# Moving a mixture-of-experts layer's row gathers between the dense matmul stages, and its bias loads into the first pass

## The chip, the cores and the metric

The kernel runs on one core of one Trainium2 chip. The metric is the time on the device in microseconds (us), as the median of three runs. A separate execution was recorded by the hardware profiler; it shows each engine's instructions and the DMA queues. In what follows PE is TensorE (matmuls), DVE is VectorE, ACT is ScalarE, POOL is GpSimd and SP is SyncE, which here only issues DMAs.

## The reference

The input `x` is 32 images of 56 x 56 positions with 128 channels, in fp32. Layer 0 adds a binarised 3 x 3 convolution of the group-normalised input to `x`. Layer 1 treats the 3136 positions of an image as tokens: it adds windowed attention (64 tokens a window, 4 heads, causal) of the normalised tokens, and then a mixture-of-experts layer in which each of the 64 experts picks its 8 best tokens of each image. Cut to what matters here:

```python
def _L1_attn_ref(x, w_qkv, w_proj, b_proj):
    qkv = xw @ w_qkv.T                      # windows of 64 tokens, 4 heads of 32
    ...
    attn = jnp.einsum('bhqd,bhkd->bhqk', q, k) * scale
    attn = jnp.where(causal, attn, NEG)
    attn = jax.nn.softmax(attn, axis=-1)
    out = jnp.einsum('bhqk,bhkd->bhqd', attn, v)
    ...
def _L1_ffn_ref(x, gate_w, gate_b, weight1, weight2):   # E = 64, K = 8, H = 512
    logits = jnp.einsum('bsd,ed->bse', x, gate_w) + gate_b
    probs = jax.nn.softmax(logits, axis=1)              # over an image's tokens
    vals, idx = jax.lax.top_k(probs.transpose(0, 2, 1), K)
    ...
    gathered = jnp.take_along_axis(x, flat_idx[:, :, None], axis=1)
    pooled = jnp.einsum('bked,bke->bed', gathered, topv)
    h = jnp.concatenate([pooled.transpose(1, 0, 2), ones], axis=-1)
    h = jax.nn.gelu(jnp.einsum('ebd,edh->ebh', h, weight1), approximate=False)
    h = jnp.concatenate([h, ones], axis=-1)
    out = jnp.einsum('ebh,eho->ebo', h, weight2)
    ...
    outputs = outputs.at[jnp.arange(Bn)[:, None], flat_idx].add(weighted)
```

The last row of each expert's `weight1` (129 x 512) and `weight2` (513 x 128) is the bias that the appended ones multiply.

## The kernel before, in words

**First pass.** SP loads all images, in 16 pairs; PE transposes them and DVE takes the statistics that the normalisations of layer 0 need (`xb`, `pt`, `st`, lines 299 to 312). Small weights are loaded and transposed ahead of it. At its end SP writes zeros to the DRAM tensor `share` (line 318), and a chain on DVE and POOL makes the thresholds `thr_a` and `thr_b` that the first convolution block needs.

**Main loop.** Two images at a time (a pair) go through in 7 blocks of 8 image rows, so 112 blocks. One iteration `n` works on several blocks at once: it runs attention of block `n` (`this`), projects queries, keys and values of `n + 1` (`nxt`), convolves `n + 4` (`conv`), and finishes block `n - 1` (`prev`). The order of the calls in the loop body is the order of instructions on every engine: the kernel declares a manual schedule for PE, DVE, ACT, SP and POOL. In an iteration PE runs, in this order: `scores` (four mask matmuls L599, then 112 small matmuls L610), four taps of the convolution (L517), the transposes L448 of `norm2` and `bits`, queries and keys (L570), `attend` (112 small matmuls L659), the gate (L723), the transposes of `norm1` (L548), `values` (L586), `turn_out` (L682), the other five taps (L517), and `project` (L692). Each small matmul of `scores` and `attend` has a weight load of its own. I call these two the dense stages: 224 instructions each.

ACT follows `scores` with two exponentials (`pT`, L625), and DVE follows `attend` with the reciprocals of the row sums (`rs`, L667). POOL raises variances to a power (L434, for `ln_rstd` and `devs`), stores the finished tokens (`out_dram`, L714), stores `ln_rstd` (`rdev`, L549) and reads it back broadcast over partitions (`rr`, L554), which DVE multiplies in at L561, in the iteration after next.

**Selection.** When a pair's seven blocks are through, its selection follows in steps, one per iteration of the next pair: `steps` holds the pairs and their step `j`. At `j` = 4 `tokens` finds the indices of the best tokens, at `j` = 5 `gather` reads their rows (eight indirect DMAs of 128 rows of 512 bytes, on POOL, L826), at `j` = 6 `row_stats` takes the rows' statistics. Step 5 falls into the fifth block of the following pair. Fifteen pairs are gathered in the loop; the last one in the tail.

**Biases.** In iteration `n` = 14 SP loads `hbias`, the hidden layer's biases, as 128 partitions x 64 experts x 4 numbers (L971), and makes four DRAM-to-DRAM copies that write the output biases, each repeated for 32 images, to `obias_d` (L977). Both are used only in the tail.

**Tail.** The experts' two layers run in eight groups, and the weighted outputs are added to the rows and scattered.

Of the kernel before, what the change touches and what calls it, by code (L numbers as in the profile page):

```python
# [8 lines left out]
F32 = mybir.dt.float32  # L9
# [5 lines left out]
ALU = mybir.AluOpType  # L15
AX = mybir.AxisListType

P = 128
# [3 lines left out]
K = 8  # L22
# [8 lines left out]
def kernel(  # L31
# [15 lines left out]
    nc = tc.nc  # L47
    B, H, W, C = x.shape
    S = H * W
    E, D1, HF = weight1.shape  # L50
# [3 lines left out]
    NHC = HF // P  # L54
    NPAIR = B // 2
    NG = E // (P // B)
    EG = P // B
# [3 lines left out]
    NU = BT // WIN  # L61
# [7 lines left out]
    const = ctx.enter_context(tc.tile_pool(name="const", bufs=1))  # L69
    dram = ctx.enter_context(tc.tile_pool(name="dram", bufs=1, space=bass.MemoryType.DRAM))  # L70
# [2 lines left out]
    share = dram.tile([NQ, P, NPAIR, 2, ES], F32, name="share")  # L73


    start = ExitStack()
    once = start.enter_context(tc.tile_pool(name="once", bufs=1, side="right"))
    ident = const.tile([P, P], F32, name="ident")
# [12 lines left out]
        out=head1, in_=head1, compare_op=ALU.is_ge, fill=0.0, base=0,  # L91
# [3 lines left out]
        out=head1, in_=head1, compare_op=ALU.is_ge, fill=0.0, base=HD - 1,  # L95
# [73 lines left out]
    with tc.tile_pool(name="prep", bufs=1) as prep, tc.tile_pool(  # L169
        name="xs", bufs=3  # L170
# [7 lines left out]
        nc.sync.dma_start(out=wp_in, in_=w_proj)  # L178
        wg_in = prep.tile([E, P], F32, name="wg_in")
        nc.sync.dma_start(out=wg_in, in_=gate_w)  # L180
        wc_in = prep.tile([P, NTAP, P], F32, name="wc_in")
        nc.sync.dma_start(out=wc_in, in_=conv_w.rearrange("kh kw i o -> i (kh kw) o"))

# [48 lines left out]
        wgc = centred(wg_in.unsqueeze(1), "wgc")  # L232
        nc.tensor.transpose(tg, wgc[:, 0, :], ident[:E, :E])
        nc.vector.tensor_copy(gateT, tg)

        wabs = prep.tile([P, NTAP, P], F32, name="wabs")
        nc.scalar.activation(wabs, wc_in, AF.Abs)
# [36 lines left out]
        def group_norm(b0, b1):  # L274

            bs = slice(b0, b1)
            mg_ps = wps.tile([P, B], F32, name="sums")
            nc.tensor.matmul(mg_ps[:, bs], lhsT=g4f, rhs=mean[:, bs], start=True, stop=True)
            nc.vector.tensor_copy(mg[:, bs], mg_ps[:, bs])
            nc.vector.tensor_sub(dev[:, bs], mean[:, bs], mg[:, bs])  # L280
            nc.vector.tensor_mul(v2[:, bs], dev[:, bs], dev[:, bs])
            nc.vector.tensor_add(v2[:, bs], v2[:, bs], var[:, bs])
            sg_ps = wps.tile([P, B], F32, name="signs")
            nc.tensor.matmul(sg_ps[:, bs], lhsT=g4f, rhs=v2[:, bs], start=True, stop=True)
            nc.vector.tensor_scalar(sg[:, bs], sg_ps[:, bs], 1e-5, None, ALU.add)
            nc.gpsimd.tensor_tensor(rg[:, bs], sg[:, bs], nhalf[:, bs], ALU.pow)
# [29 lines left out]
                scaled(0, B - 8)  # L316
        for q in range(NQ):
            nc.sync.dma_start(out=share[q].rearrange("p n i s -> p (n i s)"), in_=zero)
        group_norm(B - 8, B)
        scaled(B - 8, B)  # L320
        bmean = small("bmean", 1)
# [24 lines left out]
    grows = dram.tile([NQ, P, NPAIR, P], F32, name="grows")  # L346
    toks = [dram.tile([2, S, P], F32, name=f"toks{i}") for i in range(NPAIR)]
    eout = dram.tile([E, B, P], F32, name="eout")
    obias_d = dram.tile([P, NG, P], F32, name="obias_d")
    rdev = [dram.tile([P, NU], F32, name=f"rdev{i}") for i in range(NPAIR * NB)]  # L350
    devs = [dram.tile([2, NB * NU, WIN], F32, name=f"devs{i}") for i in range(NPAIR)]


    hbias = const.tile([P, E, NHC], F32, name="hbias")

    class Part:

# [19 lines left out]
    def main_loop(fast):  # L377
        with ExitStack() as main:
# [87 lines left out]
            class Block:  # L466
# [184 lines left out]
                def attend(self):  # L651

                    av = bank2("av")
                    for u in range(NU):
                        for h in range(HEADS):
                            for i in range(2):
                                rows = slice(i * WIN, (i + 1) * WIN)
                                m = u * 2 + h // 2
                                nc.tensor.matmul(  # L659
                                    av[h % 2 * WIN : (h % 2 + 1) * WIN, i, m * VW : (m + 1) * VW],  # L660
                                    lhsT=self.pT[h // 2][rows, h % 2, u, :],
                                    rhs=self.vb[rows, u, h, :],
                                    start=True, stop=True,
                                )
                    a = av[:, :, : 2 * NU * VW].rearrange("p i (m v) -> p i m v", v=VW)
                    rs = w2.tile([P, 2, 2 * NU], F32, name="rs")
                    nc.vector.reciprocal(rs, a[:, :, :, HD])  # L667

                    self.ao = w1.tile([P, NU, 2, 2, HD], F32, name="ao")
                    for i in range(2):  # L670
                        nc.vector.tensor_mul(
                            self.ao[:, :, i],
                            a[:, i, :, :HD].rearrange("p (u m) d -> p u m d", m=2),
                            rs[:, i].rearrange("p (u m) -> p u m", m=2)
                            .unsqueeze(3).to_broadcast([P, NU, 2, HD]),
                        )
# [52 lines left out]
            class Pair:  # L729
# [89 lines left out]
                            out=rowidx[i * ES : (i + 1) * ES, self.pr, :], in_=src[i]  # L819
                        )  # L820

                def gather(self):
                    pr, pairidx = self.pr, self.pairidx
                    self.rows = wp.tile([P, K, P], F32, name="rows")
                    for k in range(K):
                        nc.gpsimd.indirect_dma_start(  # L826
                            out=self.rows[:, k, :], out_offset=None,
                            in_=toks[pr].rearrange("i t c -> (i t) c"),
                            in_offset=bass.IndirectOffsetOnAxis(ap=pairidx[:, k : k + 1], axis=0),
                        )  # L830
# [128 lines left out]
            def at(n):  # L959
                return blocks[n] if 0 <= n < N else None  # L960

            for n in range(-7, N + 1):
# [4 lines left out]
                ends = dict(steps)  # L967
                if at(n + 7):
                    at(n + 7).load()
                if n == N // 8:  # L970
                    nc.sync.dma_start(  # L971
                        out=hbias,
                        in_=weight1[:, C : C + 1, :].rearrange("e o (p c) -> p e (o c)", c=NHC),
                    )

                    for e in range(EG):
                        nc.sync.dma_start(  # L977
                            out=obias_d[e * B : (e + 1) * B],
                            in_=weight2.rearrange("(g e) h o -> e h g o", e=EG)[e, HF : HF + 1]
                            .to_broadcast([B, NG, P]),  # L980
                        )
                if n == N - 3:
                    front.close()
                    late = main.enter_context(
# [18 lines left out]
                    nxt.normalise()  # L1003
                if at(n + 3):
                    at(n + 3).residual()
                if prev:
                    prev.norm2(pairs[prev.pr])
                if at(n + 2):
                    at(n + 2).spread1()
                if 5 in ends:  # L1010
                    ends[5].gather()
                if 7 in ends:
                    ends[7].put_rows()
                if at(n + 6):
# [5 lines left out]
                    pair.step(j)  # L1020
                if this:
                    this.attend()
                if prev:
                    prev.gate_logits(pairs[prev.pr])
                if this and this.r == NB - 1 and n < N - 1:
# [147 lines left out]
            obias = wp.tile([P, S], F32, name="drow")[:, : NG * P].rearrange("p (g o) -> p g o", o=P)  # L1173
            nc.sync.dma_start(out=obias, in_=obias_d)
            load_rows(0, 0, N1)
            pair.gather()
            other.shares(range(0, 8))
            other.store_shares()
            pair.exps()
# [85 lines left out]
```

## Time and profile before

| | us |
|---|---|
| median of 3 runs | 2330.26 |
| lowest and highest | 2326.86 to 2334.21 |
| profiled execution, its own time | 2467.31 |
| its span, first to last instruction | 2465.6 |
| PE busy in the span | 2101.3 |
| DVE busy | 1773.5 |
| ACT busy | 1147.8 |
| POOL busy | 988.5 |

The mean clock granted to TensorE in the profiled execution is 0.938 of full speed. Busy times are sums over the span; an engine can be busy with work that nobody waits for. In the lines quoted below, `x` with a number counts instructions, an arrow names what is written from what is read, and the part in brackets is the idle time before an instruction and what ended it ("issue" where the profile shows nothing that was waited for).

### The profile page before, as it was taken

The numbers are of one execution on the slowest core, as the hardware profiler recorded it, in microseconds if no ns is written. First come the engines' busy times: TensorE is split into PE (matmuls) and PEld (weight loads), VectorE is DVE, ScalarE is ACT, GpSimd is POOL, SyncE is SP. The second block draws the span as 40 slices with busy tenths as digits, with TensorE's granted clock in tenths as the row PEclk, the third lists the DMA queues.
The fourth block names the chain that finished last, engine by engine and source line by source line (L and its number), as shares of the span: only waits on it lengthen the run. The fifth ranks groups of instructions, "written<-read, shape, count | busy, mean of one in ns | idle before, by whom it ended". The sixth has DMA issues, their size and how long they took to land.

```text
span 2465.6 us, 81828 instructions
## 1 busy us (share of the span) xinstructions
PE 2101.3 (85%) x35081; PEld 1465.5 (59%) x35081; DVE 1773.5 (72%) x4974; ACT 1147.8 (47%) x1683; POOL 988.5 (40%) x996
## 2 busy tenths in 40 slices
PE   6768999799999999999999999999999999845442
PEld 5646666566666666666666666666666666523332
DVE  8966676678787878787878787878787878674221
ACT  0015555455555555555555564646565555322110
POOL 1013334243444444444444444444444444333555
PEclk9989999999999999999999999999999999867776
DMA  9973454646363636363636363636363635657762
GB/s 379 386 266 93 110 144 120 131 110 156 103 163 102 164 101 165 102 164 103 163 102 164 101 165 101 165 101 165 101 166 100 166 101 142 217 133 266 268 230 85
DMA packets 252889, 386.03 MB, mean 157 GB/s; under 512 B 56998, under 2 KB 181734, under 8 KB 247270
## 3 DMA queue, kind: packets, MB, share of 16 engines
q1 hardware_dynamic: 210150, 255.48, 36.1%
q0 software_dynamic: 40192, 124.18, 18.5%
q8 instruction: 279, 4.57, 0.8%
q10 hardware_dynamic: 2176, 1.05, 0.1%
q14 instruction: 92, 0.75, 0.1%
HBM read 246.52 MB, written 135.14 MB: 155 GB/s over the span
## 4 chain that ended last, share of the span: by engine, by line
PE 61%; DVE 12%; issue 8%; ACT 8%; POOL 5%; DMA 3%; another core or an unknown queue 2%; SPq 0%; ACTq 0%; POOLq 0%; DVEq 0%
PE pj L692 8%; PE sc L610 7%; PE av L659 6%; PE v_ps L586 6%; PE qT_ps L570 6%; PE kT_ps L570 5%; PE cv L517 4%; ACT aoT L685 4%; PE yt L548 3%; PE lg L723 3%; PE tt L448 3%; DVE st L308 3%; PE xT_ps L448 3%; POOL out_dram L1159 3%; ACT vblk L590 2%
## 5 line engine op out<-in xcount | busy, mean ns | idle before, releaser
L434 POOL TENSOR_TENSOR devs<-ln_var,nhalf 128x7 f32<-128x7 f32 x112 | 178.7, 1595 | 702.1 <-DVE ln_var L431 692.9
L625 ACT ACTIVATE pT<-sc 128x896 f32<-128x896 f32 x224 | 193.7, 916 | 370.4 <-PE sc L610 370.3
L434 POOL TENSOR_TENSOR ln_rstd<-ln_var,nhalf 128x7 f32<-128x7 f32 x112 | 174.4, 1557 | 402.8 <-DVE ln_var L431 402.5
L441 DVE BATCH_NORM_STATS2 ln_st<-tok 128x6 f32<-128x128 f32 x784 | 162.6, 279 | 183.0 <-ACT tok L709 182.7
L517 PE MATMUL cv<-hbits,wconv 128*128 128x448 f16 x1008 | 242.8, 369 | 15.5 <-DVE s L531 9.7
L659 PEld LDWEIGHTS av<-vblk,pT 64*64 64x64 f32 x12544 | 194.6, 135 | 84.5 <-ACT bn L496 68.0
L610 PE MATMUL sc<-qT,kT 32*64 32x64 f32 x12544 | 198.7, 239 | 43.9 <-issue 42.2
L610 PEld LDWEIGHTS sc<-qT,kT 32*64 32x64 f32 x12544 | 169.3, 134 | 98.7 <-issue 98.6
L692 PE MATMUL pj<-aoT,wprojT 64*128 64x448 f32 x896 | 200.3, 566 | 27.7 <-ACT aoT L685 8.9
L659 PE MATMUL av<-vblk,pT 64*64 64x33 f32 x12544 | 207.5, 221 | 11.5 <-issue 10.7
L590 ACT COPY vblk<-v_ps 128x896 f32<-128x896 f32 x112 | 101.6, 907 | 243.4 <-PE v_ps L586 241.2
L488 ACT ACTIVATE xT<-xT_ps,conv_nb 128x896 f32<-128x896 f32 x112 | 114.1, 1019 | 174.9 <-PE xT_ps L448 166.2
L570 PE MATMUL qT_ps<-n1T,wqkvT 128*128 128x448 f32 x448 | 191.9, 552 | 2.9 <-DVE n1T L561 2.7
L586 PE MATMUL v_ps<-wqkvT,n1T 128*128 128x128 f32 x1568 | 193.5, 275 | 0.0
L570 PE MATMUL kT_ps<-n1T,wqkvT 128*128 128x448 f32 x448 | 188.4, 543 | 0.0
L441 DVE BATCH_NORM_STATS2 ln_st<-yt 128x6 f32<-128x128 f32 x784 | 165.5, 281 | 31.8 <-PE yt L548 27.4
L586 PEld LDWEIGHTS v_ps<-wqkvT,n1T 128*128 128x128 f32 x1568 | 185.2, 193 | 0.7 <-issue 0.7
L701 DVE SCALAR_TENSOR_TENSOR tT<-pj,bproj_c,yT 128x448 f32<-128x448 f32 x224 | 142.7, 678 | 48.7 <-PE pj L692 47.7
L714 POOL DMA_DIRECT2D out_dram<-tok x224 | 170.0, 761 | 0.0
L1159 POOL DMA_INDIRECT out_dram<-f_rows,rowidx x128 | 123.9, 968 | 101.6 <-DVE f_rows L1155 65.0
L826 POOL DMA_INDIRECT rows<-toks,pairidx x128 | 138.5, 1082 | 46.0 <-issue 38.1
L727 ACT COPY logits<-lg 128x448 f32<-128x448 f32 x112 | 59.8, 534 | 203.3 <-PE lg L723 203.3
(190 smaller groups left out, 4162.1 us busy)
## 6 DMA issues: line engine op xcount, KB each, us to landing
xb<-in_x_dram SPq DMA_DIRECT2D x16, 3136.0 KB
xb<-in_x_dram SPq DMA_DIRECT2D x224, 224.0 KB
rr<-rdev POOLq DMA_DIRECT2D x112, 448.0 KB
toks<-tok SPq DMA_DIRECT2D x224, 224.0 KB
out_dram<-tok POOLq DMA_DIRECT2D x224, 224.0 KB
u<-in_L_ffn_weight_dram SPq DMA_DIRECT2D x16, 2048.0 KB
drow<-devs SPq DMA_DIRECT2D x94, 224.0 KB
share<-zero SPq DMA_DIRECT2D x8, 1024.0 KB
```

Source lines behind the costliest of these rows:

```text
L434: nc.gpsimd.tensor_tensor(rstd, var, nhalf[:, :n], ALU.pow)
L441: nc.vector.bn_stats(st[:, u, :], src[:, u, :])
L517: nc.tensor.matmul(self.cv[:, :BT], lhsT=wconv[:, t, :], rhs=hb[:, r * RB + kh : r * RB + kh + RB, kw : kw + W], start=(t == 0), stop=(t = ...
L570: nc.tensor.matmul(pp[:, a, :BT], lhsT=wqkvT[:, s, :], rhs=flat[:, a * BT : (a + 1) * BT], start=True, stop=True,)
L586: nc.tensor.matmul(units(vp)[:, u, :], lhsT=self.n1T[:, u, :], rhs=wqkvT[:, 2, :], start=True, stop=True,)
L590: nc.scalar.copy(self.vb[:, :, :, :HD], units(vp).rearrange("p u (h d) -> p u h d", d=HD))
L610: nc.tensor.matmul(tiles[h // 2][part, h % 2, u * WIN : (u + 1) * WIN], lhsT=left[hp, u, part], rhs=right[hp, u, part], start=False, stop= ...
L625: nc.scalar.activation(pT, rows2(sc), AF.Exp, scale=HD ** -0.5)
L659: nc.tensor.matmul(av[h % 2 * WIN : (h % 2 + 1) * WIN, i, m * VW : (m + 1) * VW], lhsT=self.pT[h // 2][rows, h % 2, u, :], rhs=self.vb[row ...
L692: nc.tensor.matmul(pj[:, i, :BT], lhsT=wprojT[rows, g, :], rhs=self.aoT[rows, :, g, :], start=(g == 0), stop=(g == 1),)
L714: q.dma_start(out=to[part, :].rearrange("(u t) c -> t u c", t=WIN), in_=tok[i * WIN : (i + 1) * WIN],)
L1159: put = nc.gpsimd.indirect_dma_start(out=of, out_offset=bass.IndirectOffsetOnAxis(ap=rowidx[:, n, q : q + 1], axis=0), in_=rows[q][:, n, : ...
```

## The change

The eight gathers of step 5 are issued in two groups of four. The first group moves up, ahead of `norm2`, and POOL first runs a new operation `seen` that reads one column of `pT[0]`, so the group can't start before the first exponential of this iteration is done. The second group stands behind `attend`, and its `seen` reads one column of `rs`. In the tail all eight are issued together, without `seen`. The hidden layer's biases are loaded at the start of the first pass as rows of experts, transposed by four matmuls and copied to `hbias`. The four copies to `obias_d` are issued behind the zeroing of `share`. The loop no longer loads either.

```diff
+    obias_d = dram.tile([P, NG, P], F32, name="obias_d")
+    hbias = const.tile([P, E, NHC], F32, name="hbias")
...
+        hb_in = prep.tile([E, P, NHC], F32, name="hb_in")
+        nc.sync.dma_start(
+            out=hb_in.rearrange("e p c -> e (p c)"), in_=weight1[:, C, :]
+        )
         wc_in = prep.tile([P, NTAP, P], F32, name="wc_in")
...
+        th = wps.tile([P, NHC, E], F32, name="th", tag="tw")
+        for c in range(NHC):
+            nc.tensor.transpose(th[:, c, :], hb_in[:, :, c], ident[:E, :E])
+        nc.vector.tensor_copy(hbias.rearrange("p e c -> p c e"), th)
...
         for q in range(NQ):
             nc.sync.dma_start(out=share[q].rearrange("p n i s -> p (n i s)"), in_=zero)
+        for e in range(EG):
+            nc.sync.dma_start(
+                out=obias_d[e * B : (e + 1) * B],
+                in_=weight2.rearrange("(g e) h o -> e h g o", e=EG)[e, HF : HF + 1].to_broadcast([B, NG, P]),
+            )
...
-                    rs = w2.tile([P, 2, 2 * NU], F32, name="rs")
+                    rs = self.rs = w2.tile([P, 2, 2 * NU], F32, name="rs")
...
-                def gather(self):
+                def gather(self, ks, behind=None):
                     pr, pairidx = self.pr, self.pairidx
-                    self.rows = wp.tile([P, K, P], F32, name="rows")
-                    for k in range(K):
+                    if behind is not None:
+                        seen = wp.tile([P, 1], F32, name="seen")
+                        nc.gpsimd.tensor_scalar(seen, behind, 0.0, None, ALU.mult)
+                    if ks[0] == 0:
+                        self.rows = wp.tile([P, K, P], F32, name="rows")
+                    for k in ks:
                         nc.gpsimd.indirect_dma_start(
...
-                if n == N // 8:
-                    nc.sync.dma_start(
-                        out=hbias,
-                        in_=weight1[:, C : C + 1, :].rearrange("e o (p c) -> p e (o c)", c=NHC),
-                    )
-                    for e in range(EG):
-                        nc.sync.dma_start(
-                            out=obias_d[e * B : (e + 1) * B],
-                            in_=weight2.rearrange("(g e) h o -> e h g o", e=EG)[e, HF : HF + 1]
-                            .to_broadcast([B, NG, P]),
-                        )
...
                 if at(n + 3):
                     at(n + 3).residual()
+                if 5 in ends:
+                    ends[5].gather(range(0, K // 2), this.pT[0][:, 0, 0, 0:1])
                 if prev:
                     prev.norm2(pairs[prev.pr])
                 if at(n + 2):
                     at(n + 2).spread1()
-                if 5 in ends:
-                    ends[5].gather()
...
                 if this:
                     this.attend()
+                if 5 in ends:
+                    ends[5].gather(range(K // 2, K), this.rs[:, 0, 0:1])
                 if prev:
                     prev.gate_logits(pairs[prev.pr])
...
-            pair.gather()
+            pair.gather(range(K))
```

More of the change, by code (lines that the diff above doesn't have):

```diff
@@ L348 @@
     eout = dram.tile([E, B, P], F32, name="eout")
-    obias_d = dram.tile([P, NG, P], F32, name="obias_d")
     rdev = [dram.tile([P, NU], F32, name=f"rdev{i}") for i in range(NPAIR * NB)]
     devs = [dram.tile([2, NB * NU, WIN], F32, name=f"devs{i}") for i in range(NPAIR)]
-    hbias = const.tile([P, E, NHC], F32, name="hbias")
     class Part:
```

## The prediction

> **What bounds the kernel now.** I read the page first, for the engine that carries the span:
>
> ```profile
> PE 2101.3 (85%) x35081; PEld 1465.5 (59%) x35081; DVE 1773.5 (72%) x4974; ACT 1147.8 (47%) x1683; POOL 988.5 (40%) x996
> PE 61%; DVE 12%; issue 8%; ACT 8%; POOL 5%; DMA 3%; another core or an unknown queue 2%; SPq 0%; ACTq 0%; POOLq 0%; DVEq 0%
> L826 POOL DMA_INDIRECT rows<-toks,pairidx x128 | 138.5, 1082 | 46.0 <-issue 38.1
> ```
>
> TensorE bounds the span. The gathers (L826) cost 138.5 us of POOL, which is 40% busy, so by their own time they are free. But 8% of the chain is "issue": TensorE stood still and the profile names no releaser. To find where, I cut the loop at the first mask matmul of each iteration (L599 in the timeline) and asked for busy time by stretch. These are five iterations in a row, the third, fourth, fifth, sixth and seventh block of a pair. The columns are length, then PE, PEld, DVE, ACT and POOL busy, then the clock granted:
>
> ```profile
> 984.80:1001.00 16.20, 16.11 (x303) 11.18 (x301) 13.94 (x35) 9.29 (x12) 6.02 (x7) 1.00 0.43 116
> 1001.00:1018.40 17.40, 16.20 (x303) 11.19 (x301) 14.73 (x42) 9.32 (x12) 5.80 (x7) 1.00 0.44 109
> 1018.40:1035.30 16.90, 15.99 (x303) 11.14 (x301) 13.11 (x39) 9.23 (x12) 9.12 (x11) 1.00 0.46 125
> 1035.30:1057.30 22.00, 19.09 (x301) 12.94 (x299) 14.41 (x49) 9.94 (x13) 13.95 (x13) 0.92 0.45 117
> 1057.30:1074.30 17.00, 16.18 (x304) 11.24 (x302) 14.17 (x48) 11.93 (x16) 6.56 (x8) 1.00 0.58 139
> ```
>
> An iteration lasts 16.2 us, with TensorE full. The fourth line lasts 22.0 with no more matmuls and a clock of 0.92. The gathers begin in the iteration before it (POOL 9.12) and end in it. Over the 15 pairs gathered inside the loop this iteration lasts 21.7 to 24.0 us; against 16.2 the 15 add up to 94 us. The timeline shows where the time goes (start, length, engine, line):
>
> ```profile
> 1031.77 0.38 PE L682 MATMUL aoT_ps<-ident,ao 128*128 128x128 f32 x2
> ...
> 1036.11 0.92 PE L610 MATMUL sc<-qT,kT 32*64 32x64 f32 x32
> ...
> 1038.84 0.34 PE L610 MATMUL sc<-qT,kT 32*64 32x64 f32 x5 [0.38 <-issue]
> 1039.60 0.95 POOL L826 DMA_INDIRECT rows<-toks,pairidx  x1 [0.30 <-issue]
> ...
> 1041.11 1.11 PE L610 MATMUL sc<-qT,kT 32*64 32x64 f32 x60 [0.40 <-issue]
> 1042.15 1.67 PE L517 MATMUL cv<-hbits,wconv 128*128 128x448 f16 x4
> ```
>
> Undisturbed, the 112 score matmuls take 1.5 us. Here 32 go through at speed, then 5 or so per 0.74 us (7 per us) while gathers run, then the last 60 at speed once the last gather has ended (1040.55). The scores lose 4.7 us; the rest of the 5.8 is the clock, halved afterwards (the four L517 matmuls take 1.67 against 0.94). Stages of few, long matmuls (L682, L517, L692) keep their times beside the gathers: only the two dense stages, scores (L610) and attend (L659), are open to this.
>
> Last I looked for single long iterations. There is one, 29.7 us from 458.6, behind the loads of the biases (L971, L977):
>
> ```profile
> 466.26 0.89 PE L659 MATMUL av<-vblk,pT 64*64 64x33 f32 x44
> 476.81 2.14 PE L659 MATMUL av<-vblk,pT 64*64 64x33 f32 x68 [9.66 <-issue]
> ...
> 445.01 12.53 SPq L977 DMA_DIRECT2D obias_d<-in_L_ffn_weight_dram  x4
> ...
> 456.00:462.00 6.00, 5.87 (x140) 3.53 (x139) 5.89 (x11) 2.95 (x5) 2.15 (x2) 1.00 0.34 40
> 462.00:468.00 6.00, 5.15 (x65) 3.27 (x63) 3.93 (x15) 5.33 (x7) 2.25 (x2) 1.00 0.66 44
> ```
>
> TensorE stops within attend for 9.7 us. The trace's record of its instruction queue has a block that was due and started only at 474.5. The queues move 40 to 44 GB/s at that time, a tenth of what they move in the first pass. This iteration lost 13.4 us and the one before 1.4: 14.8 together.
>
> **The change, part by part.** The sum is made against the profiled execution, 2467.3 us (span 2465.6). The median of the runs shown is 2330.3, 137 us or 5.6% less; I scale the result by 2330/2467 = 0.944 and return to this gap in the rivals.
>
> *Gathers leave the scores.* Removed per pair: 22.15 (the median) less what remains. That iteration keeps its row statistics (L849, eight of 0.2 us on DVE, which is 14.4 of 22 busy), so I set 16.5: 5.6 us.
>
> *First group, behind the first exponentials.* In the undisturbed iteration that starts at 1018.38 the exponentials run from 1020.75, two of 0.87: the first ends at 1021.6. POOL is idle from 1019.5 to 1025.45 there, so the new POOL operation starts at once. Its row is not in the trace. Below: POOL's memset of one column, 0.10; above: POOL's power on one column, 0.56. I take 0.5, with 0.3 for its wait: 1022.4, and 0.3 more to the first gather. Eight gathers took from 1029.41 to 1040.55, 1.39 each; four end at 1028.0. Attend starts at 1026.03: 32 matmuls at speed to 1026.6, then 7 per us until 0.5 after the last gather (14 by 1028.5), then 66 at 112 per 1.83 us (1.1): it ends at 1029.6 instead of 1027.86. Cost 1.75 us; 0.9 at 1.25 per gather, 2.5 if it starts 0.7 later. The half clock would add 1.2; I leave it out, because attend stopped for 1.3 us at 450.5 and the clock stayed at 1.00.
>
> *What is queued behind it on POOL.* The `devs` power (L434) moves from 1025.45 to 1028.0, then two output stores (1.51) and the broadcast of `rr` (L554), from 1028.5 to 1031.1. Its reader is the product of L561 in the next iteration, at about 1039. A broadcast issued at 531.95 had its last packets at about 536, 4.3 us later; 1035.4 is early enough. ACT must not overwrite `pT`, nor DVE `rs`, until POOL has read them; both have two buffers and are written an iteration later. Cost nothing; if that cover were gone, up to 2.6 us per pair.
>
> *Second group, behind the reciprocals.* `rs` is ready by 1030.0, POOL free at 1031.7, gathers from 1032.9 to 1038.2. The next scores would start at 1036.11 + 1.75 = 1037.9, so their first 32 matmuls cover the rest: 0.3 us. `ln_rstd` and its store end at about 1040.7; the broadcast that needs them comes at about 1047. The 0.7 that the third line above has over 16.2 (ACT's copy of L685 late beside the gathers) stays.
>
> Per pair 5.6 - 1.75 - 0.3 = 3.55; by 15: **-53 us**. The last pair's gather, in the tail, is as before.
>
> A rule speaks against this. The Trainium skill, SBUF — State Buffer, "Who interferes with whom" and the part before it, says that a transfer issued from POOL can't write its descriptors while DVE runs an operation that holds the port they share, and stretches from 0.6 to 3.1 us. The first group lies beside DVE's statistics and bits. At 3.1 each, four end at 1035: attend would lose over 7 us and the gain be gone. The row: gathers beside DVE's L701, L561 and L538 (540 to 544) took 0.94 to 1.29 each, and the longest of all 1.89. I go by the row.
>
> *Biases of the hidden layer.* Instead of 8192 pieces of 16 bytes, 64 rows of 2 KB ahead of `wc_in`, four transposes (0.1 to 0.2 each) and one copy of 256 columns from PSUM (L211, 256 columns: 0.41). They stand right before the first statistics of a pass that DVE bounds (18.96 of 20 us busy from 138 to 158): **+0.8 us**.
>
> *Biases of the output* (L977): the same four copies, now between the zeroing of `share` and the first block's load on SP's queue. What held the instructions up at 466? The Trainium skill, Perfetto Trace Analysis, "DMA Optimizations", says that transfers below 2 KB carry a large overhead each; by this rule the 16-byte pieces are the culprit, and the change wins 14.8 at no cost. In the trace the 16-byte load has landed at 456.6, ten us before the stop; the four copies land at 462.8, 469.5, 472.8 and 475.3. So the stop belongs to the copies, and they only move: **-14.8** here, and about 19 us of copying at the start:
>
> ```profile
> 138.00:158.00 20.00, 16.55 (x116) 13.21 (x116) 18.96 (x37) 0.00 (x0) 0.00 (x0) 0.94 0.96 404
> 163.81 2.79 PE L448 MATMUL xT_ps<-ident,xb 128*128 128x128 f32 x14 [0.56 <-DVE sg L285]
> ...
> 169.00 1.34 ACT L496 ACTIVATE bn<-xT_ps,thr_b,thr_a 128x448 f32<-128x448 f32 x2 [2.79 <-DVE thr_b L339]
> ```
>
> The zeros keep the queue full (404 GB/s) to about 158.7, and the first blocks land by 162, just in time. With the copies between, block 0 lands at 158.7 + 19 + 2 = 180; transposes 1.5 and ACT's copy 1.0 put the first `bn` at 183 instead of 169: **+14 us**. Bounds: +5 if the copies go twice as fast, +22 at 40 GB/s for all of the 1.05 MB.
>
> Sum: -53 + 0.8 - 14.8 + 14 = -53 of 2467; scaled -50, hence 2280.
>
> **The rivals.**
> (1) *The start cost is real and the stalls are not* (slower). Where does the timed run save 137 us? Iterations of 16.2 us hold 16.1 of TensorE; there is little to save. The stalls of the profiled execution (94 + 14.8 = 109 us) would be the place, if starving the matmuls' issue is something that recording them causes. Then moving gathers is worth nothing, no stop is removed, and 14 us come on top: 2330 + 14, up to 22. It decides as soon as less than a quarter of the 53 + 14.8 is in the timed run. Against it: the slow supply follows the gathers to half a us, and the tail (285 us, clock 0.5 to 0.7) can hold a share of the 137.
> (2) *Part of the stalls is in the timed run*: a quarter to a half; the two sides cancel: 2320 to 2337.
> (3) *Attend takes over more*: gathers start later than I think and the half clock comes in: 2.5 + 1.2 per pair instead of 1.75, 15 x 1.95 = 29 more; -53 + 29 = -24, scaled -23: 2307.
>
> **How the numbers follow.** The forecast, with (3) at its edge, has 0.60 and its own range 2252 to 2307 (attend at 0.9 and start at +5 on one side). Rival (2) 0.18, rival (1) 0.22. 0.3%, 7 us, is about what a measurement of this kernel can tell from no change: faster 0.60, same 0.18, slower 0.22. The range 2252 to 2344 leaves out half of (1) and a few in a hundred below.
>
> **What would show it.** After, the sixth iteration of a pair should last about 16.5 with the clock at 1.00, the fifth about 18.6 with attend near 3.6 us; no stop at 466; the first `bn` near 183; the granted clock's mean up by about 0.02. Wrong: scores still in groups of five, an attend of over 6 us, `rr` waited for in L561, or the profiled span 50 us shorter while the timed median has not moved.

## The result, and the profile after

| | us | ratio to before |
|---|---|---|
| before, 20 runs | 2330.27 (2321.77 to 2339.28) | |
| after, 20 runs | 2324.58 (2319.64 to 2331.46) | 0.9976 [0.9966, 0.9985] |
| after, profiled execution, its own time | 2323.97 | |

The change gains 5.7 us, 0.24%, where 50 were forecast. The profiled execution of after agrees with its timed runs; that of before had stood 137 us above its own. First, from the page of after, the same three lines as were shown of before:

```profile
PE 2051.1 (88%) x35085; PEld 1437.5 (62%) x35085; DVE 1774.3 (76%) x4975; ACT 1145.4 (49%) x1683; POOL 997.4 (43%) x1026
PE 60%; DVE 14%; ACT 9%; DMA 6%; issue 5%; POOL 4%; SPq 1%; ACTq 0%; POOLq 0%; DVEq 0%
L846 POOL DMA_INDIRECT rows<-toks,pairidx x128 | 131.6, 1028 | 45.1 <-issue 36.7
```

TensorE has 50 us less of busy time with the same matmuls and four transposes more, and "issue" fell from 8% to 5% of the chain. The POOL line is that of the gathers, now 1.03 us each. The windows of after cut the same five iterations of a pair at the first mask matmul (columns as before). Ahead of them stand two stretches of the start, and behind them the tail from the first matmul of the experts (L1105, `hp`) to the end:

```profile
158.00:170.00 12.00, 4.60 (x32) 3.58 (x32) 8.40 (x27) 0.00 (x0) 2.02 (x2) 0.84 0.63 163
170.00:180.00 10.00, 0.00 (x0) 0.00 (x0) 1.80 (x10) 0.00 (x0) 1.03 (x2) 0.50 0.79 115
...
950.07:966.25 16.18, 16.09 (x302) 11.18 (x300) 13.92 (x35) 9.30 (x12) 5.99 (x7) 1.00 0.43 116
966.25:983.63 17.38, 16.18 (x301) 11.18 (x299) 14.71 (x42) 9.32 (x12) 5.76 (x7) 1.00 0.43 110
983.63:1000.23 16.60, 16.44 (x302) 11.43 (x300) 12.34 (x38) 9.22 (x12) 11.55 (x15) 1.00 0.51 132
1000.23:1016.49 16.26, 16.13 (x302) 11.21 (x300) 15.15 (x50) 9.88 (x13) 11.45 (x11) 1.00 0.57 144
1016.49:1033.41 16.92, 16.11 (x302) 11.21 (x300) 14.08 (x48) 11.90 (x16) 6.50 (x8) 1.00 0.57 145
...
2125.60:2322.20 196.60, 103.36 (x704) 74.55 (x704) 56.90 (x122) 46.35 (x256) 125.23 (x130) 0.76 0.75 264
```

The sixth iteration (1000.23) lasts 16.26 us instead of 22.00, with the clock at 1.00. By the two profiles alone (spans of 2465.6 and 2322.2) the change looks like a gain of 143 us. This is the last of the signs of being wrong that the prediction lists: the profiled span 50 us shorter while the timed median has not moved. Here it is 143 us shorter, and the median moved by 5.7. The timeline says why the reading fails:

```profile
183.19 3.22 PE L463 MATMUL xT_ps<-ident,xb 128*128 128x128 f32 x14 [17.32 <-DMA xb<-in_x_dram]
...
185.91 1.33 ACT L511 ACTIVATE bn<-xT_ps,thr_b,thr_a 128x448 f32<-128x448 f32 x2
...
987.02 0.24 POOL L842 TENSOR_SCALAR seen<-pT 128x1 f32<-128x1 f32 x1 [2.27 <-ACT pT L640]
988.01 1.08 POOL L846 DMA_INDIRECT rows<-toks,pairidx  x1 [0.75 <-issue]
...
990.67 1.07 POOL L846 DMA_INDIRECT rows<-toks,pairidx  x1 [0.30 <-issue]
991.28 2.33 PE L674 MATMUL av<-vblk,pT 64*64 64x33 f32 x112
992.05 0.95 POOL L846 DMA_INDIRECT rows<-toks,pairidx  x1 [0.30 <-issue]
...
2243.57 1.24 DVE L1143 TENSOR_TENSOR os<-op,drow 32x128 f32<-32x128 f32 x4 [0.54 <-PE op L1137]
```

The first group starts at 988.01, as forecast 4.4 us into the iteration, and two of its gathers lie beside `attend` (L674). In the forecast's picture that costs 1.75 us: `attend` stalls, and takes 3.6 us. Here all 112 matmuls go through in one piece, in 2.33 us against about 1.84 undisturbed. So in this execution the gathers cost `attend` 0.5 us. Something else than the change must tell the profile of before from that of after.

### The profile page after: what moved, and what is told of

Its sections match the earlier page's. It is cut to its first block, busy times and chain, and to the rows that moved or that the text cites. A ratio compares the mean times of both kernels' runs of the same rounds, so it can differ in the third digit from the quotient of the medians.

```text
span 2322.2 us, 81869 instructions
## 1 busy us (share of the span) xinstructions
PE 2051.1 (88%) x35085; PEld 1437.5 (62%) x35085; DVE 1774.3 (76%) x4975; ACT 1145.4 (49%) x1683; POOL 997.4 (43%) x1026
## 4 chain that ended last, share of the span: by engine, by line
PE 60%; DVE 14%; ACT 9%; DMA 6%; issue 5%; POOL 4%; SPq 1%; ACTq 0%; POOLq 0%; DVEq 0%
PE pj L707 7%; PE av L674 6%; PE sc L625 6%; PE v_ps L601 6%; PE qT_ps L585 5%; PE kT_ps L585 5%; ACT aoT L700 4%; PE yt L563 4%; PE cv L532 3%; PE lg L738 3%; DVE st L322 3%; PE xT_ps L463 3%; PE tt L463 3%; ACT vblk L605 3%; DVE idx L809 2%
## 5 line engine op out<-in xcount | busy, mean ns | idle before, releaser
L674 PEld LDWEIGHTS av<-vblk,pT 64*64 64x64 f32 x12544 | 197.2, 135 | 76.3 <-ACT bn L511 69.2
L532 PE MATMUL cv<-hbits,wconv 128*128 128x448 f16 x1008 | 232.3, 357 | 10.2 <-DVE s L546 8.6
L605 ACT COPY vblk<-v_ps 128x896 f32<-128x896 f32 x112 | 101.6, 907 | 242.6 <-PE v_ps L601 242.6
L707 PE MATMUL pj<-aoT,wprojT 64*128 64x448 f32 x896 | 200.3, 566 | 17.1 <-ACT aoT L700 5.4
L674 PE MATMUL av<-vblk,pT 64*64 64x33 f32 x12544 | 211.5, 221 | 1.7 <-ACT bn L511 0.6
L625 PEld LDWEIGHTS sc<-qT,kT 32*64 32x64 f32 x12544 | 154.3, 130 | 45.9 <-issue 45.2
L716 DVE SCALAR_TENSOR_TENSOR tT<-pj,bproj_c,yT 128x448 f32<-128x448 f32 x224 | 142.7, 678 | 47.8 <-PE pj L707 47.7
L625 PE MATMUL sc<-qT,kT 32*64 32x64 f32 x12544 | 170.6, 233 | 3.4 <-issue 3.4
L846 POOL DMA_INDIRECT rows<-toks,pairidx x128 | 131.6, 1028 | 45.1 <-issue 36.7
L511 ACT ACTIVATE bn<-xT_ps,thr_b,thr_a 128x448 f32<-128x448 f32 x224 | 150.8, 735 | 0.0
```

The lines of the kernel that those rows point to most:

```text
L511: nc.scalar.activation(bn[:, i].rearrange("c h (g j) -> c h g j", j=NU), units(xT_ps)[:, :, i * WIN : (i + 1) * WIN].rearrange("c j (h g) ...
L532: nc.tensor.matmul(self.cv[:, :BT], lhsT=wconv[:, t, :], rhs=hb[:, r * RB + kh : r * RB + kh + RB, kw : kw + W], start=(t == 0), stop=(t = ...
L605: nc.scalar.copy(self.vb[:, :, :, :HD], units(vp).rearrange("p u (h d) -> p u h d", d=HD))
L625: nc.tensor.matmul(tiles[h // 2][part, h % 2, u * WIN : (u + 1) * WIN], lhsT=left[hp, u, part], rhs=right[hp, u, part], start=False, stop= ...
L674: nc.tensor.matmul(av[h % 2 * WIN : (h % 2 + 1) * WIN, i, m * VW : (m + 1) * VW], lhsT=self.pT[h // 2][rows, h % 2, u, :], rhs=self.vb[row ...
L707: nc.tensor.matmul(pj[:, i, :BT], lhsT=wprojT[rows, g, :], rhs=self.aoT[rows, :, g, :], start=(g == 0), stop=(g == 1),)
```

## The experiments

Theories. **A**: the stalls occur only where an execution is recorded (the reason of the prediction's rival 1). **D**, formed from the first runs: there are two conditions of the machine, and a recorded execution takes what timed runs take in the same one. Below, "quicker condition" means that the kernel before takes about 2330 us in timed runs beside the kernel tested, "slower condition" that it takes 2460 to 2473. The runs fell on five chips: chip 12 was in the quicker condition, chips 7, 1, 10 and 11 in the slower one. By their times the 40 runs of the table above are of the quicker condition too, and the profile of before (2467) is of the slower one. In each cut of a kernel below, `...` stands for lines left out.

**Chip 12: the parts of the change one by one** (before: 2329.57).

e1_gathers: the gathers in two groups alone; both loads of the biases as before.

```diff
+                    ends[5].gather(range(0, K // 2), this.pT[0][:, 0, 0, 0:1])
...
+                    ends[5].gather(range(K // 2, K), this.rs[:, 0, 0:1])
```

> The kernel before with the gathers in two groups alone; the biases stay in the loop. Theory A (the stalls of the scores belong to the recorded execution): the profiled span falls by 90 us or more, the timed run moves by no more than 6 us (2324 to 2331). Theory B (the stalls are in the timed runs too, and the start of the loop takes the gain back in the changed kernel): the timed run falls by 20 us or more, to 2310 or below.

Measured: 2324.37, ratio 0.9982 [0.9971, 0.9992], 5.2 us less. The recorded span is 2321.3, 144 us below that of before. Both numbers are what theory A expected, so by itself this run speaks for A. Of the single long iteration behind the biases this execution's timeline has

```profile
469.83 2.13 PE L661 MATMUL av<-vblk,pT 64*64 64x33 f32 x68 [11.38 <-issue]
```

So the stop that the prediction found there is real in the quicker condition too: this iteration and the one before it take 47.8 us together, in after 33.2.

e2_biases: both moves of the biases alone; eight gathers together, as before (the edit is shown against after).

```diff
                     at(n + 2).spread1()
+                if 5 in ends:
+                    ends[5].gather(range(K))
```

> The kernel before with both bias loads moved to the first pass; the gathers stay in one group of eight. Theory A: the profiled span still has the scores at 6 us per gathered pair, its stop at 466 is gone and its first bn comes at 183 to 186; the timed run is within 4 us of before if the stop within attend is in the timed run, and 14 us slower (2344) if it isn't. Theory B: the timed run is 15 us slower or more, so that the gathers' gain and this make the -6 us of both together.

Measured: 2329.28, ratio 0.9998 [0.9986, 1.001]: no change. Gain and cost cancel: the long iteration is gone (33.2 us for the two), and the first mask matmul starts at 221.4 us instead of 204.1 in e1. This execution is also the nearest to a profile of the old gathers in the quicker condition. The sixth iteration in its windows, and the gathers beside the scores (L625) in its timeline:

```profile
1002.01:1018.52 16.51, 16.38 (x302) 11.40 (x299) 15.23 (x50) 9.85 (x13) 14.55 (x14) 1.00 0.55 144
```

```profile
1002.38 1.00 POOL L846 DMA_INDIRECT rows<-toks,pairidx  x1 [0.30 <-issue]
...
1002.86 1.87 PE L625 MATMUL sc<-qT,kT 32*64 32x64 f32 x112
1003.68 0.95 POOL L846 DMA_INDIRECT rows<-toks,pairidx  x1 [0.31 <-issue]
```

The eight gathers lie where they lay before, beside the scores, and the 112 matmuls take 1.87 us against about 1.5 undisturbed. The iteration lasts 16.5 us, not 22; without any gathers (e6_none below) it lasts 16.24. So of the 5.6 us per pair at most 0.3 was there to win. It also speaks against theory A, which expected scores of 6 us in any recording with the gathers in one group.

e4_spread: after, with the four copies to `obias_d` back in the loop, one each in iterations 16, 23, 30 and 37 (the edit is shown against after).

```diff
-        for e in range(EG):
-            nc.sync.dma_start(out=obias_d[e * B : (e + 1) * B], ...
...
+                if n in OB:
+                    e = OB.index(n)
+                    nc.sync.dma_start(out=obias_d[e * B : (e + 1) * B], ...
```

> The changed kernel with the four copies of the output biases taken out of the start of the loop: one each in iterations 16, 23, 30 and 37. If the 14 to 17 us that the start lost in the profile are in the timed run as well, this is 14 us faster than the changed kernel: 2311 timed, and the first bn at 172 in the profile. If the start cost is only in the recorded execution, 2325. If copies in the loop stop the matmuls wherever they stand, each costs up to 3.5 us and the gain is nil.

Measured: 2315.85, ratio 0.9939 [0.9918, 0.996], 13.7 us less than before and the shortest median of all. The first mask matmul starts at 207.6 instead of 219.5, so the copies at the start cost 12 us; a quarter of them in one iteration costs 1 to 2 us in two of the four iterations (17.36 and 18.38 us against 16.16 and 16.47) and nothing in the others.

e6_none: no gathers in the loop.

```diff
+                    if pr < NPAIR - 1:
+                        nc.gpsimd.memset(self.rows, 0.0)
-                    for k in range(K):
+                    for k in range(K if pr == NPAIR - 1 else 0):
```

> The kernel before without the gathers in the loop: the rows of fifteen pairs are set to zero by one POOL memset in the same place (the last pair still gathers), so the output lacks what those rows give. It bounds what any placing of the gathers can win. Theory A: the timed run falls by less than 6 us although the profiled span loses 90 or more. Theory B: the timed run falls by 20 us or more.

Measured: 2317.72, ratio 0.9959 [0.9943, 0.9974]. All 120 gathers of the loop together cost 11.9 us here (6 to 13 by the interval), 0.1 each. That is the ceiling for any way of moving them in this condition; the two groups of e1 win 5.2 of it.

**Chip 7: before is another kernel here** (before: 2460.21).

b2_before and b3_before are the kernel before, unchanged.

> The kernel before, recorded once more, with nothing changed. With the gathers in one group of eight the kernel of the biases alone had a recorded span of 2331, no more than its timed run, so a third theory (C): the first recorded execution of the kernel before was not like its other executions. C: this span is within 10 us of 2330, the sixth iteration of a pair lasts 16.5 us, the stop within attend is still there. Theory A (recording slows the gathers' neighbours): 2440 to 2470 again, with the scores at 6 us.

> The same kernel a third time, for the spread of recorded executions. Theory C: within 10 us of 2330. Theory A: 2440 to 2470.

Measured: 2458.97 and 2453.74, recorded; the timed runs beside them took 2456 to 2467. Not recorded and yet 130 us longer than on chip 12: theory A falls. Theory C falls with it, since the first recorded execution was like these two. D took shape.

e3_hbias: the hidden layer's biases in the first pass; the four copies of the output biases and the gathers stay as in before.

> The kernel before with the hidden layer's biases loaded and transposed in the first pass, the four copies of the output biases still in iteration 14, the gathers in one group. If the copies are what stops the matmuls, the stop of 13 us stays and the timed run is that of before (2329, within 3). If the 16-byte pieces are, the stop is gone and the timed run is 12 to 15 us faster (2315 to 2318).

Measured: 2454.09, ratio 0.9963 [0.9947, 0.9979], 6.1 us less: neither of the two outcomes that were expected. The long iteration lasts 24.1 us, against 29.5 and 30.3 in the two recordings of before on this chip (29.5 to 34.6 in all six), and TensorE stops for 6.4 us in it, now in the scores:

```profile
465.90 1.25 PE L620 MATMUL sc<-qT,kT 32*64 32x64 f32 x60 [6.42 <-issue]
```

So without the load in 16-byte pieces this iteration is 5 to 6 us shorter than on the same chip before, and the copies alone make the rest of the stop. Whether the pieces hold TensorE up themselves, or only hold up the copies behind them, is not shown: no run has the pieces without the copies.

What ends the stop can be read in the traces. They show the fetches of TensorE's instruction blocks, of 16384 bytes each. In all fifteen recordings that have the four copies in iteration 14, no fetch starts for 18 to 24 us, and TensorE resumes 2.2 to 2.5 us after the next one has started (before: 474.47 and 476.81; e3: 463.48 and 465.90). The longest other pause between two fetches in the loop of before is 14.5 us. So the stop looks like a wait for a late block of instructions. That is read from the traces, not tested, and what delays the fetch is not shown.

e5_twice: before with seven more gathers in each of the 15 pairs.

```diff
+                    if pr < NPAIR - 1:
+                        again = wp.tile([P, K - 1, P], F32, name="again")
+                        for k in range(K - 1):
+                            nc.gpsimd.indirect_dma_start(out=again[:, k, :], ...
```

> The kernel before with seven more gathers behind the eight of each pair in the loop, into a tile that nothing reads. If gathers slow the matmuls beside them in ordinary executions as in the first recorded one, 7 gathers more cost about 5 us a pair: 75 us timed. If each gather costs what taking all eight away won (12 us over 15 pairs, 0.1 us a gather), 7 more cost about 10 us. If nothing, 2330.

Measured: 2610.67, ratio 1.0608 [1.059, 1.0627]: 150.5 us for 105 gathers, 1.43 each, in timed runs. That is twice the 75 us expected where gathers slow the matmuls.

**Chip 1: the changed kernel in the slower condition** (before: 2470.39). a2_after is after, unchanged; b4_before is before; e5b_twice and e6b_none repeat e5_twice and e6_none.

> The changed kernel again, beside the kernel before on the same chip. The kernel before was 2330 us on the chip of the first four experiments and 2460 on that of the second four, and its recorded spans (2466, 2457, 2452) are those of the second. Theory D: there are two conditions of the machine. In the first the gathers don't touch the matmuls, and the change wins 6 us (ratio 0.9976); in the second they do, and the change wins what the prediction's sum said or more: 53 us of the scores, the stop and the tail's pauses stay or go (2460 to 2350 or below, ratio 0.98 or lower). If the kernel before is 2330 here, this is 2324; if 2460, 2310 to 2400.

> The kernel before, recorded on this chip. Theory D: the span is within 10 us of the timed runs of this chip; if these are 2330, the sixth iteration of a pair lasts 16.5 us and the tail from its first hidden layer about 198 us; if 2460, 22 and 236.

> Seven more gathers for each of fifteen pairs, as before: where the kernel before took 2460 they cost 150 us, 1.4 us a gather, as long as a gather lasts. Theory D: where the kernel before takes 2330 they cost 0 to 12 us.

> The kernel before without the gathers in the loop (rows of fifteen pairs set to zero). Where the kernel before took 2330 this won 12 us. Theory D: where it takes 2460, this wins about 95 us from the loop (22.2 to 16.2 us in fifteen iterations) and keeps the tail's pauses: 2365.

Measured: a2_after 2425.05, ratio 0.9803 [0.978, 0.9827], **45.3 us less than before** (a little less of a gain than the 2310 to 2400 expected). b4_before 2469.07, e5b_twice 2622.33 (1.0603 [1.0575, 1.0631]), e6b_none 2369.96 (0.9582 [0.9552, 0.9613]): here the gathers of the loop cost 100 us instead of 12.

e6b_none and e6_none are the same kernel, recorded in both conditions. Their fifteen fifth iterations sum to 240.0 us (slower) and 240.3 (quicker), their sixth to 242.6 and 242.5, and the stop of the biases is in both (51.4 and 51.2 us for the two iterations). Their tails take 246.2 and 198.4. So without gathers the loop is the same in both conditions, and only the tail, with its indirect stores, still differs.

The windows of a2_after are those of after in the other condition, fifth and sixth iteration and the tail:

```profile
1000.12:1023.03 22.91, 19.15 (x301) 12.95 (x299) 14.21 (x40) 9.22 (x12) 16.06 (x18) 0.88 0.42 105
1023.03:1039.73 16.70, 16.57 (x301) 11.24 (x299) 13.56 (x47) 9.85 (x13) 7.46 (x7) 0.96 0.51 128
...
2181.00:2424.10 243.10, 104.95 (x704) 76.50 (x704) 57.09 (x123) 46.56 (x256) 125.66 (x130) 0.69 0.62 213
```

The fifth iteration is 6.3 us longer than in after (it is the longest of the 15; their median is 18.80), and the tail as it is cut here, whose code the change doesn't touch, is 46 us longer with nearly the same busy times. The timeline of a2_after, first with `attend` (L674) in the same place as in after, then two lines of the tail:

```profile
1007.16 1.08 POOL L846 DMA_INDIRECT rows<-toks,pairidx  x1 [0.30 <-issue]
1007.77 0.79 PE L674 MATMUL av<-vblk,pT 64*64 64x33 f32 x40
1008.55 0.95 POOL L846 DMA_INDIRECT rows<-toks,pairidx  x1 [0.30 <-issue]
1009.07 0.34 PE L674 MATMUL av<-vblk,pT 64*64 64x33 f32 x5 [0.51 <-issue]
...
1010.52 2.13 PE L674 MATMUL av<-vblk,pT 64*64 64x33 f32 x67 [1.12 <-issue]
...
1020.71 3.29 PE L707 MATMUL pj<-aoT,wprojT 64*128 64x448 f32 x8 [2.13 <-ACT aoT L700]
...
2335.77 1.24 DVE L1143 TENSOR_TENSOR os<-op,drow 32x128 f32<-32x128 f32 x4 [8.05 <-remote]
...
2343.00 1.29 DVE L1110 COPY hs<-hp 128x512 f32<-128x512 f32 x2 [5.98 <-remote]
```

Here is the pattern that the prediction read in the scores of before: some 40 matmuls, then 5, then the rest. The gathers themselves are the same: 1.4 us from one to the next in both executions. In the tail, beside the indirect stores, even DVE stands for 6 to 8 us, which ends by something the profile can't name ("remote"); in after the line of L1143 waited 0.54 us. Over the whole tail DVE has 29 pauses of more than 2 us, 152 us in all; in after it has 9, of 86.

**Chip 10: does a plain load do the same** (before: 2468.77). b5_before is before, e4b_spread is e4_spread, e5c_twice is e5_twice. e7_plain is e6_none with seven plain loads of as many bytes from POOL in the place of the gathers:

```diff
+                        plain = wp.tile([P, K - 1, P], F32, name="plain")
+                        for k in range(K - 1):
+                            nc.gpsimd.dma_start(
+                                out=plain[:, k, :],
+                                in_=toks[pr].rearrange("i t c -> (i t) c")[k * P : (k + 1) * P],
+                            )
```

> The kernel before, unchanged, recorded once. Theory D (the condition belongs to the machine that a run lands on, and a recorded execution takes what a timed run takes there): the recorded time lies within 5 us of the timed runs of the kernel before on the same chip, whichever they are: near 2330 with a sixth iteration of 16.5 us and no stretch at half clock, or near 2460 with one of 22 us and 15 such stretches. Theory A (recording causes the stalls): 2460 with a sixth iteration of 22 us, whatever the timed runs take.

> The kernel before, in which the rows of the 15 pairs gathered in the loop are set to zero (one POOL memset each) and seven plain loads of 128 consecutive rows of 512 bytes, issued from POOL, take the place of the gathers; they land in a tile that nobody reads. Same queue, same bytes per load, no indices. Where the kernel before takes about 2460 us: if the traffic, or the writing of descriptors for any POOL transfer, starves TensorE, the sixth iteration lasts 21 to 22 us and the time is that of before; if it is what an indirect transfer does besides, the sixth iteration lasts about 16.3 us and the time is 90 to 100 us less, as without gathers. Where the kernel before takes about 2330: the sixth iteration 16.3 to 16.5 and 0 to 12 us less under both.

> The changed kernel with the four copies of the output biases one each in iterations 16, 23, 30 and 37, as before (on the chip where before took 2329.57 it took 2315.85). Where before takes about 2460 to 2470: the start cost of 14 us goes, and a copy of 0.26 MB in an iteration should cost less than the stop of 13.4 for all four, so 8 to 14 us less than the changed kernel's 2425: 2411 to 2417. Where before takes about 2330: 2313 to 2319 again.

> The kernel before with seven more gathers in each of the 15 pairs of the loop, into a tile that nobody reads. Theory D: where before takes about 2330, gathers do not starve TensorE, so the 105 more cost only what shares POOL and the queues, 0 to 15 us (2330 to 2345), and the sixth iteration stays at 16.3 to 17.5 us. If the condition only set how deep the stalls are, and each gather still cost a part of 1.43 us, 20 to 80 us. Where before takes about 2460: 2600 to 2625 as on the other two chips.

Measured: b5_before 2470.43. e7_plain 2365.54, ratio 0.9584 [0.9559, 0.9608]; e5c_twice 2622.59 (1.0628 [1.0607, 1.0649]); e4b_spread 2416.72 (0.9796 [0.9766, 0.9826]). The sixth iterations of b5_before and of e5c_twice, from the windows of each:

```profile
1034.47:1056.40 21.93, 19.02 (x301) 12.82 (x299) 14.51 (x49) 9.97 (x13) 14.05 (x13) 0.92 0.44 112
```

```profile
1084.46:1116.69 32.23, 23.44 (x301) 15.69 (x299) 14.64 (x49) 10.10 (x13) 20.79 (x20) 0.79 0.37 98
```

Seven more gathers add 10.3 us to the one iteration and pull its clock down to 0.79. e7_plain took 103 us less than before, as if there were no gathers, but it does not tell bytes from indices, as its timeline shows:

```profile
987.86 1.84 PE L659 MATMUL av<-vblk,pT 64*64 64x33 f32 x112
988.85 1.53 POOL L714 DMA_DIRECT2D out_dram<-tok  x2
...
991.86 3.84 POOL L829 DMA_DIRECT2D plain<-toks  x7
...
997.16 1.46 PE L610 MATMUL sc<-qT,kT 32*64 32x64 f32 x112
```

The seven loads take POOL 3.84 us, 0.55 each, and are through before the scores begin (their last packets end at 997.0): they lay beside no dense stage. Only the store ahead of them (L714, 224 KB) lies partly beside one, and that `attend` takes its usual 1.84 us. This experiment is inconclusive. e4b_spread gains as much as a2_after beside its own before; the intervals overlap, so the copies' place is not settled in this condition.

**Chip 11** (before: 2472.6). b6_before is before, e5d_twice is e5_twice.

> The kernel before, unchanged, recorded once more, on whichever chip it falls. Theory D: the recorded time lies within 5 us of the timed runs of before there. Near 2330: a sixth iteration of 16.5 us and no stretch at half clock in the loop. Near 2460 to 2470: 22 us and 15 such stretches. Theory A (recording causes the stalls): 2460 or more, also where the timed runs take 2330.

> The kernel before with seven more gathers in each of the 15 pairs of the loop, as on three chips of the slower condition (2611 to 2623 there). Theory D: where before takes about 2330, gathers do not starve TensorE, so 105 more cost 0 to 15 us: 2330 to 2345. If the condition only sets how deep the stalls are: 20 to 80 us more. Where before takes 2460 to 2470: 2610 to 2625 again.

Measured: 2471.55, and 2625.34 (1.0634 [1.0606, 1.0663]). A fourth chip with the slower condition, of the same size.

**What stays open.** What causes the two conditions: all runs on one chip shared one of them, which fits a property of the chip, but each chip was met once, so time or placement isn't excluded. No recording of the kernel before, and no run with doubled gathers, fell on a chip of the quicker condition. By what path an indirect transfer holds TensorE's instructions back isn't shown either, nor whether plain transfers beside a dense stage would do the same. In the profile of before, the fetches of instruction blocks around the stall start at 1032.86 and 1042.47, and issue resumed at 1041.11, so this stall, unlike the stop of the biases, didn't end with the landing of such a block.

## Why the prediction was wrong

Each step against what was measured. "Slower" is a2_after against b4_before on chip 1, both recorded; "quicker" is e1, e2 and after. An iteration is cut at the first weight load of its mask matmuls.

| step | forecast | slower | quicker |
|---|---|---|---|
| *Gathers leave the scores*: 15 sixth iterations | -84 | 337.1 to 243.5: -93.6 | 247.1 (e2) to 243.8 (e1): -3.3 |
| *First* and *second group*: 15 fifth iterations | +31 | 250.8 to 296.6: +45.8 | 241.0 (e2) to 247.6 (e1): +6.6 |
| gathers, sum | -53 | -47.8 | timed, e1: -5.2 |
| *stop* of the biases | -14.8 | 50.2 to 33.3: -16.9 | 47.8 (e1) to 33.2: -14.6 |
| start of the loop (with +0.8) | +14.8 | 204.2 to 221.0: +16.8 | 204.1 (e1) to 219.5: +15.4 |
| whole | -53, scaled -50 | timed: -45.3 | timed: -5.7 |

In the quicker column the first two rows add to +3.3, where e1 gained 5.2 in timed runs. The seventh iterations, which no step of the forecast names, differ by 10.8 us the other way (250.0 in e2, 239.2 in e1), so these recordings don't show where the 5.2 were won.

- **The step that failed** is "I scale the result by 2330/2467 = 0.944". It took a profile from one condition and timed runs from the other as the same execution up to a factor. The gap of 137 us was no 5.6% spread over everything. Between b5_before (slower) and e2 (quicker), whose spans differ by 138.0, the sixth iterations differ by 336.6 - 247.1 = 89.5 us, the fifth by 9.6 and the tail by 47.4, together 146.5; the moved biases and the seventh iterations make the rest, -8.5. The undisturbed iterations last 16.2 us in both. In the slower condition, for which the sum was made, it came near (-45.3 timed against -53). The cost that the change removes was itself most of the gap, so what remained to be won was near nothing.
- **The step's premise stood in the text.** Rival (1) asked where the timed run could save 137 us, and answered: in the stalls. That was right. Its reason (recording causes them) was wrong, and its sum was too: it took the stop of the biases out together with the gathers' stalls, and ended at 2344. The stop is there in both conditions, pays for the later start, and so the time stayed just below before. Rival (2) had that time in its range, 2320 to 2337, but for another reason, that a quarter to a half of the stalls is in the timed run; it was near by luck.
- **Gathers leave the scores**: right in mechanism and size where the condition holds (22.22 to 16.12, the medians of b4_before and a2_after; 16.5 forecast).
- **First group**: undersized there, most of all by the clock. `attend` took 4.0 to 5.0 us where 3.6 was forecast, and 2.1 to 2.5 in after. In eight of the fifteen fifth iterations of a2_after the granted clock stayed at 1.00, and these last 17.1 to 18.8 us, near the 18.6 forecast. In the other seven it is 0.88 to 0.92, and they last 20.2 to 22.9. So the half clock, left out on the ground of one stop (1.3 us in the text, 1.09 by its row), did come in. Rival (3) had put 3.7 per pair on this step, and 45.8/15 is 3.1. **Second group**: put at 0.3, but in the two longest fifth iterations ACT's copy of L700 is late beside it, and `project` (in the longest L707 at 1020.71) waits 2.13 us for it and takes 3.29 instead of 1.77.
- **Queued on POOL**: put at nothing, and no row contradicts it: DVE waits for `rr` 15 times in a2_after, 12.5 us in all, and 14 times in b5_before, 14.6 us. The `seen` operation took 0.2 to 0.8 us where 0.5 was taken.
- **Start**: first `bn` at 183 forecast, 185.91 measured; TensorE has no instruction from 170 to 180 and waits 17.32 us for `xb`. Right within 3 us.
- **Biases**: the stop went, as forecast, but "the stop belongs to the copies" was right only in part: without the 16-byte pieces e3 is 5 to 6 us shorter there. So the rule on small transfers that the prediction set aside (the Trainium skill, Perfetto Trace Analysis, "DMA Optimizations") may have a part in it, though no run has the pieces alone. The copies fall under the same rule, since their packets in the trace have 512 bytes.
- **The rule on the shared port** (the Trainium skill, SBUF — State Buffer, "Who interferes with whom"), set aside as well, stays unseen: the sixty gathers of the first groups in after took 0.95 to 1.14 us each, not 3.1.

## What to carry to other kernels

Before a profile's stall is worth anything, hold the profiled execution's own time against the timed runs: where they differ by more than their spread, the stalls may be the difference, as most of it was here, and scaling the sum by the ratio of the two is no remedy. The indirect loads issued from POOL cost this kernel 0.1 us each in one condition of the machine and 0.8 to 1.4 in the other, where they hold up dense stages of small matmuls, so keep them out of such stages, and judge it on more than one chip. The DRAM-to-DRAM copies cost least one at a time in the loop, as far as the quicker condition shows it: the version that spreads them, e4_spread, is 13.7 us (0.6%) quicker than before in the quicker condition. In the slower one it is 52 us (2%) quicker, most of it by the gathers.

## What the runs showed of the hardware that was not expected

- The same kernel takes 2330 us on one chip and 2460 to 2473 on four others. Nearly all of the difference lies beside indirect transfers: 120 gathers cost 11.9 us on the first and 100.4 on chip 1, and the tail with its indirect stores 197 to 200 against 236 to 247.
- In the slower condition each further gather costs 1.43 us (150.5/105; 1.45 to 1.47 on the three other chips), about the 1.3 us from one gather to the next: nearly all its time is lost to TensorE. Part of that is the clock, 0.79 in the iteration with fifteen gathers.
- Behind the four copies in one iteration TensorE stands for 6.4 to 12.1 us, in all fifteen recordings that have them there and in both conditions, until 2.2 to 2.5 us after the fetch of its next block of instructions (16384 bytes) has started.
